# A drain of GpSimd behind every gather in a graph layer

## The chip, the cores and the metric

The kernel runs on one core of a Trainium2 chip. The metric is the device time of one execution in microseconds (us); the number that counts is the median of several executions.

## The reference

A graph of 6250 nodes with 64 features each and 206250 edges, sorted by their target node. Each node's row is normalised and clipped at zero (`h`); each edge takes its source's row of `h`, adds its own 64 attributes and clips again; the results are summed per target node, and a two-layer network with a residual closes the layer.

```python
h = jnp.maximum(_layernorm(x, axis=-1), 0.0)
# _L0_gnn_ref(h, edge_index, edge_attr, W1, b1, W2, b2):
msg = jax.nn.relu(h[src] + edge_attr)                       # 206250 x 64
agg = jax.ops.segment_sum(msg, dst, num_segments=6250)      # dst is sorted
y = jax.nn.relu((h + agg) @ W1 + b1) @ W2 + b2
out = x + y
```

## The kernel before, in words

The edges are cut into groups of 768 (128 partitions by 6 columns). Groups from the sixth on are taken in 144 **sets** of one or two groups; a set is the unit of the main loop `both_units(k)`, which lasts some 8 us. The source rows `h[src]` of a set come in two ways:

- **A little over half of the columns by matmuls.** VectorE (DVE) builds zero-one matrices (`found`, L564, and `backs`, L574), TensorE (PE) multiplies them with the table of nodes held on the chip (`across_of` L594, `turn_of` L604, `pick` L618, `decode_sum` L690), and ScalarE (ACT) copies the results out of PSUM in between (L599, L612, L683).
- **The others by gathers.** GpSimd (POOL in the profile) issues indirect DMAs from `gather` (L226): one instruction for each column, which fetches 128 rows of 64 floats out of `h_rows` in DRAM by the indices in `src_sb` and puts them into a tile `xg`. Sets of one group have no gathered column; the others have six. The first five groups are gathered whole: 18 gathers of raw rows of `x` and 12 of `h_rows`, into the tiles `xr`.

`decode(k)` adds both kinds of rows to the edges' attributes (L698 for the picked ones, L701 for the gathered ones), `messages` clips them (L708), `window_sum` (L722) sums them by target node, and `sum_into_z` (L645) adds the sums to `z`. Every so often 512 nodes go through the two-layer network (L748, L758).

The order on each engine is the order in which the code is written (a manual schedule). Two mechanisms set when a gather may start. One is written out: `fetch_next(it)` is called from inside `pick` and issues the next gather of a list `pending`, with a dependency on the matmul `it` just issued, so that the gathers are strewn among the matmuls of the main loop. The list begins nine sets ahead of the set at work (`AHEAD = 9`), and the tiles `xgs` are a ring of 11 sets. The other comes from the framework: a gather's landing is told by one of eight semaphores taken in turn, and a wait for the gather eight places earlier stands ahead of each gather as an event semaphore on POOL's sequencer.

```python
            if (u * H + t) % 2 == q // QW and q % QW == QW - 1 and (u * H + t) % (2 * H) < 2 * H - 1:
                fetch_next(it)
```

A last branch of the program (from L1114 on) handles edges that fit no window, gathers included; it is not taken with these inputs.

Of the kernel before, what the change touches and what calls it, by code (L numbers as in the profile page):

```python
# [80 lines left out]
def kernel(  # L81
# [14 lines left out]
    nc = tc.nc  # L96
# [129 lines left out]
    def gather(xg, idx, n, rows, behind=()):  # L226

        for j in range(n):
            it = nc.gpsimd.indirect_dma_start(  # L229
                out=xg[:, j, :], out_offset=None, in_=rows[:, :],  # L230
                in_offset=bass.IndirectOffsetOnAxis(ap=idx[:, j:j + 1], axis=0))
            if j >= n - len(behind):
                tc.add_manual_dep(it.ins, behind[j - n + len(behind)].ins.name, beat, reason="pace")

# [6 lines left out]
    def fetch(g, behind=()):  # L241
        lo, hi = first_col(g), pool_cols(g)
        if hi:
            gather(rows_of(g)[:, lo:], src_sb[:, g * G + lo:g * G + hi], hi - lo, x if g < RAW else h_rows, behind[lo:])
# [18 lines left out]
    def fetch_next(behind):  # L263
        if pending:
            g, j = pending.pop(0)
            gather(rows_of(g)[:, j:], src_sb[:, g * G + j:], 1, h_rows, [behind])
# [847 lines left out]
    with tc.If(any_left > 0):  # L1114
        nc.gpsimd.iota(wide, pattern=[[1, WB]], base=1, channel_multiplier=0, allow_small_or_imprecise_dtypes=True)
        with tc.For_i(0, NG, 1) as i:
            idx = work.tile([P, G], I32, name="idx")
            lf = work.tile([P, G], F32, name="lf")
            nc.vector.tensor_copy(idx, src_sb[:, ds(i * G, G)])
            nc.vector.tensor_copy(lf, left[:, ds(i * G, G)])  # L1120
            ea = eas[0][:, 0]
            nc.sync.dma_start(out=ea.rearrange("p j d -> p (j d)"),
                              in_=edge_attr[ds(i * GE, GE), :].rearrange("(p j) d -> p (j d)", j=G))
            xa = xgs[0].rearrange("p g j d -> p (g j) d")
            gather(xa, idx, G, h_rows)
            all_windows(combine(xa, ea, G), lf, G)
        ea = eas[0][:, 0]
        attr_load(ea, NG)
        xa = xgs[0].rearrange("p g j d -> p (g j) d")
        gather(xa[:, G - CT:], src_sb[:, CP - CT:], CT, h_rows)  # L1130
        all_windows(combine(xa[:, G - CT:], ea[:, G - CT:], CT), left[:, CP - CT:], CT)

        for c in range(NB + 1):
            o, xb = result(c, *hidden(c))
            base_rows(c, xb)
            store(c, o, xb)
# [39 lines left out]
```

## Time and profile before

| | |
|---|---|
| median of 3 runs | 1317.23 us (1314.55 to 1322.07) |
| the profiled execution | 1329.39 us |
| its span, first to last instruction | 1327.7 us |
| granted TensorE clock, mean | 0.918 |
| busy: PE, DVE, ACT, POOL | 1041.3, 855.2, 853.0, 764.3 us |
| gathers executed | 748 (18 + 12 into `xr`, 718 into `xg`) |

In the profile's rows a group of instructions stands as: line, engine, operation, tile written and tiles read, count; then busy time and the mean duration of one in ns; then the idle time of the engine just ahead of them and what ended it. A name with a "q" behind it (POOLq) is the engine's sequencer, which waits, branches and issues; its records are not counted as busy. A gather's record on POOL is the time in which GpSimd works on it, not the time until its rows have landed.

### The profile page before, as it was taken

To read this page: it belongs to the slowest core of one execution; us is meant where nothing else is said; L and a number is where in the kernel's file an instruction comes from. 1 tells how busy PE (TensorE), PEld (TensorE's weight loads), DVE (VectorE), ACT (ScalarE), POOL (GpSimd) and SP (SyncE) were. 2 spreads that over 40 slices of the span, in tenths; PEclk is the share of its full clock that TensorE was granted. 3 is DMA by queue.
4 is the path that set the end of the run, shared out by engine and by line. 5 is a ranking of instruction groups with operands and counts; after the bars stand their busy time and mean duration, and the time that the engine had idled before them with its cause. 6 is when DMAs were issued, how large, how long until landed. Compare 5 with 4: busy or idle time off the path is not lost. (4 is left out here: it accounts for less than half of the span.)

```text
span 1327.7 us, 39109 instructions
## 1 busy us (share of the span) xinstructions
PE 1041.3 (78%) x15593; PEld 925.0 (70%) x15593; DVE 855.2 (64%) x2167; ACT 853.0 (64%) x1849; POOL 764.3 (58%) x763
## 2 busy tenths in 40 slices
PE   0235888878887887888888888888888887888897
PEld 0224777777776777777777777777777776777796
DVE  8672766666576676576566665665666765766684
ACT  3334666666666666666666666666666666666685
POOL 7674665655565665565565565655566666566510
PEclk9767988989999999899998998989889999999898
DMA  5222444444444444444444444444444444444441
GB/s 187 81 60 93 141 134 128 144 134 122 144 138 135 146 139 134 142 119 134 130 139 140 137 138 127 138 129 139 137 139 141 139 138 141 138 139 141 127 127 55
DMA packets 92790, 173.72 MB, mean 131 GB/s; under 512 B 23673, under 2 KB 61178, under 8 KB 92602
## 3 DMA queue, kind: packets, MB, share of 16 engines
q1 hardware_dynamic: 68554, 146.58, 33.4%
q0 software_dynamic: 23936, 24.56, 9.3%
q8 instruction: 124, 2.03, 0.6%
q14 instruction: 64, 0.52, 0.2%
q10 hardware_dynamic: 112, 0.03, 0.0%
HBM read 167.22 MB, written 3.87 MB: 129 GB/s over the span
## 5 line engine op out<-in xcount | busy, mean ns | idle before, releaser
L229 POOL DMA_INDIRECT xg<-h_rows,src_sb x718 | 730.9, 1018 | 494.1 <-PE pick L618 209.3
L618 PE MATMUL pick<-picked,backs 128*128 128x128 f16 x5184 | 412.2, 230 | 35.3 <-issue 33.8
L618 PEld LDWEIGHTS <-backs 128*128 128x128 f16 x5184 | 329.8, 103 | 61.1 <-issue 50.3
L612 ACT CAST picked<-half 128x512 f16<-128x512 f32 x432 | 249.1, 577 | 177.8 <-remote 53.2
L698 DVE SCALAR_TENSOR_TENSOR ea<-pick,ea 128x192 f32<-128x192 f32 x288 | 101.7, 354 | 401.6 <-PE pick L722 108.1
L599 ACT CAST across<-half 128x512 f16<-128x512 f32 x432 | 253.7, 587 | 158.7 <-PE pick L618 57.4
L594 PE MATMUL half<-found,hp 128*128 128x128 f16 x3456 | 288.4, 229 | 22.9 <-issue 19.9
L594 PEld LDWEIGHTS <-hp 128*128 128x128 f16 x3456 | 233.8, 103 | 39.5 <-issue 31.0
L574 DVE TENSOR_SCALAR backs<-spots,ids 128x1536 f16<-128x1536 int16 x432 | 255.2, 637 | 0.0
L722 PE MATMUL pick<-oh,ea 128*64 128x32 f32 x3176 | 143.2, 226 | 82.1 <-issue 60.2
L722 PEld LDWEIGHTS pick<-oh,ea 128*64 128x64 f32 x3176 | 117.8, 138 | 118.3 <-issue 88.1
L604 PE MATMUL half<-ident_h,across 128*128 128x128 f16 x1728 | 179.4, 229 | 18.0 <-ACT across L599 13.7
L683 ACT CAST both<-pick 128x384 f16<-128x384 f32 x288 | 140.1, 486 | 62.9 <-issue 17.6
L564 DVE TENSOR_SCALAR found<-sources,nodes_of 128x1536 f16<-128x1536 int16 x288 | 170.3, 638 | 9.7 <-issue 9.7
L604 PEld LDWEIGHTS <-across 128*128 128x128 f16 x1728 | 131.0, 103 | 27.2 <-ACT across L599 14.4
L708 ACT ACTIVATE ea<-ea 128x768 f32<-128x768 f32 x144 | 114.5, 795 | 0.7 <-DVE ea L701 0.7
L684 ACT ACTIVATE minus<-both 128x192 f16<-128x192 f16 x288 | 104.5, 363 | 9.1
L655 DVE TENSOR_TENSOR oh<-slot,pick 128x384 f32<-128x384 int16 x144 | 74.0, 514 | 0.3 <-PE pick L690 0.3
L690 PE MATMUL pick<-both,weigh_high 128*128 128x192 f16 x288 | 72.6, 252 | 0.2 <-ACT both L683 0.2
L690 PE MATMUL pick<-minus,weigh_sign 128*128 128x192 f16 x288 | 72.3, 251 | 0.4 <-issue 0.3
L690 PE MATMUL pick<-both,ident_h 128*128 128x192 f16 x288 | 72.5, 252 | 0.0
L690 PE MATMUL pick<-minus,weigh_last 128*128 128x192 f16 x288 | 72.0, 250 | 0.0
(135 smaller groups left out, 809.1 us busy)
## 6 DMA issues: line engine op xcount, KB each, us to landing
sources<-source_row SPq DMA_DIRECT2D x72, 768.0 KB
ea<-in_edge_attr_dram SPq DMA_DIRECT2D x118, 384.0 KB
spots<-spot_rows SPq DMA_DIRECT2D x72, 384.0 KB
xg<-h_rows,src_sb POOLq DMA_INDIRECT x718
ea<-in_edge_attr_dram SPq DMA_DIRECT2D x32, 192.0 KB
xb<-in_x_dram SPq DMA_DIRECT2D x12, 128.0 KB
out_dram<-o SPq DMA_DIRECT2D x12, 128.0 KB
h_rows<-x SPq DMA_DIRECT2D x3, 384.0 KB
```

What stands on the lines that cost most here:

```text
L229: it = nc.gpsimd.indirect_dma_start(out=xg[:, j, :], out_offset=None, in_=rows[:, :], in_offset=bass.IndirectOffsetOnAxis(ap=idx[:, j:j + ...
L564: nc.vector.tensor_scalar(found[d][:, b * PARTS + m:b * PARTS + m + PARTS // 2].rearrange("p m u s -> p (m u s)"), sources[d][:, m * 4 * S ...
L574: nc.vector.tensor_scalar(backs[d][:, q, w].rearrange("p t s -> p (t s)"), spots[d].bitcast(I16), ids[:, w * QW + q:w * QW + q + 1], None, ...
L594: last = nc.tensor.matmul(ps[:, j * P:(j + 1) * P], hp[:, b * PARTS + m].rearrange("p t d -> p (t d)"), found[d][:, b * PARTS + m].rearran ...
L599: nc.scalar.copy(across[d, q].rearrange("p u j s -> p j u s"), ps.rearrange("p (j u s) -> p j u s", j=J, u=4))
L604: last = nc.tensor.matmul(ps[:, u * P:(u + 1) * P], ac[:, u].rearrange("p j s -> p (j s)"), ident_h, start=True, stop=True)
L612: nc.scalar.copy(picked[d][:, q].rearrange("p u d -> p (u d)"), turned.pop((d, q)))
L618: it = nc.tensor.matmul(ps[:, :, t], backs[d][:, q % QW, q // QW, u * H + t, :], picked[d][:, q, u].rearrange("p (w d) -> p w d", w=2), st ...
L683: nc.scalar.copy(both[:, i], picks_of(k, i))
L690: nc.tensor.matmul(picks_of(k, i)[:, 0], weights, rows, start=(j == 0), stop=(j == len(terms) - 1))
L708: nc.scalar.activation(msg, msg, AF.Relu)
L722: last = nc.tensor.matmul(pa[i * D:(i + 1) * D], msg[:, j, :], oh[:, j, :], start=(j < lo + 2), stop=(j >= G - 2))
```

## The change

Behind every indirect DMA that `gather` issues, a drain is put into GpSimd's instructions: a step of its sequencer that is meant to wait until the engine has finished the instructions before it. All calls of `gather` are affected: the 748 that run and the ten in the branch that is not taken. The semaphores, the waits, the dependencies of the pace and the order of all other instructions on all engines stay as they were; the drains themselves wait for no semaphore and set none.

```diff
@@ def gather(xg, idx, n, rows, behind=()):
             it = nc.gpsimd.indirect_dma_start(
                 out=xg[:, j, :], out_offset=None, in_=rows[:, :],
                 in_offset=bass.IndirectOffsetOnAxis(ap=idx[:, j:j + 1], axis=0))
+            nc.gpsimd.drain()
             if j >= n - len(behind):
                 tc.add_manual_dep(it.ins, behind[j - n + len(behind)].ins.name, beat, reason="pace")
```

## The prediction

> **What bounds the kernel now.** I read the page first, for shares and for the chain that ended last.
>
> ```profile
> span 1327.7 us, 39109 instructions
> PE 1041.3 (78%) x15593; PEld 925.0 (70%) x15593; DVE 855.2 (64%) x2167; ACT 853.0 (64%) x1849; POOL 764.3 (58%) x763
> PE 39%; issue 7%; ACT 2%; DVE 1%; DMA 0%; DVEq 0%; POOL 0%; ACTq 0%
> ```
>
> The third row is the chain by engine. It was followed back over only half of the span (its shares sum to 49%), but in that half PE holds 39 of 49 and POOL nothing. PE is the bound, with the engines that feed it out of PSUM; POOL, which the change touches, is busy for 58% and off the path. So the question is how far POOL can be slowed before somebody waits for its gathers. Next I read POOL's one large group in the main loop alone (121 to 1268.5 us), and the page of the gather's line, in which the last two rows are those who waited for it.
>
> ```profile
> L229 POOL DMA_INDIRECT xg<-h_rows,src_sb x676 | 686.2, 1015 | 471.8 <-PE pick L618 209.3 <-issue 77.6 <-PE half L604 68.4
> L229 POOL DMA_INDIRECT xg<-h_rows,src_sb x718: 938/944/1732, 43.6 to 1267.4; - x180
> L229 POOLq EVENT_SEMAPHORE  x699: 17/17/3868, 27.0 to 1265.6; - x175
> ...
>   ACT raw_sq L630: 5.9, 1
>   POOL xr L229: 0.6, 2
> ```
>
> 676 gathers of 1015 ns make 686.2 us of work in that stretch, and POOL idles 471.8 us ahead of them, mostly because the pace (the pick at L618 and its neighbours) has not let the next one go. Nobody in the main loop is shown waiting for a gather; the two rows of waiters lie in the first 60 us. How early the gathers are is read from their reader, the addition at L701:
>
> ```profile
> L701 DVE SCALAR_TENSOR_TENSOR ea<-xg,ea x120: 544/559/568, 133.8 to 1316.3; 128x384 f32<-128x384 f32 x120
> ...
>   issue: 0.6, 2
> ```
>
> Idle time of DVE ahead of 120 of these is 0.6 us in all. Now the ends of the loop on POOL's timeline (start, duration, what, idle time ahead of it), and a step of the chain that shows a gather's landing:
>
> ```profile
> 51.64 0.94 POOL L229 DMA_INDIRECT xg<-h_rows,src_sb  x1 [1.62 <-DVE raw_v L633]
> ...
> 109.34 0.94 POOL L229 DMA_INDIRECT xg<-h_rows,src_sb  x1 [0.30 <-issue]
> 121.07 1.54 POOL L229 DMA_INDIRECT xg<-h_rows,src_sb  x1 [10.79 <-PE pick L618]
> ...
> 1151.08 0.95 POOL L229 DMA_INDIRECT xg<-h_rows,src_sb  x1 [0.30 <-issue]
> 1152.33 0.94 POOL L229 DMA_INDIRECT xg<-h_rows,src_sb  x1 [0.31 <-issue]
> ...
> 1267.40 0.94 POOL L229 DMA_INDIRECT xg<-h_rows,src_sb  x1 [0.45 <-PE pick L690]
> ```
>
> ```profile
> 1151.08 3.33 DMA xg<-h_rows,src_sb
> ```
>
> The gather at 51.64 is the sixth into `xg`, the last one that the first L701 (133.8) needs: it ended 81 us early. The last one ends at 1268.34 and the last L701 starts at 1316.3: 48 us early. A gather lands some 3.33 us after its start, 2.4 after its end, so the cushion is 79 us at first and 45.6 at the end. And two gathers that wait for nothing stand 0.30 us apart: already now they don't overlap.
>
> **The change, part by part.** It adds 748 drains to POOL's sequencer and touches nothing else. Behind a drain are queued the next event semaphore (the 17 ns row) and the next gather; who waits for those is L701 alone, with the cushion above.
>
> *The price of one drain.* No drain behind a gather is in the trace; these are the drains there are, with the last of four MEMSETs that the first of them stands behind:
>
> ```profile
> L1162 POOLq DRAIN  x1: 188/188/188, 0.4 to 0.4; - x1
> ...
> 0.41 0.12 POOL L1162 MEMSET const-uint8-127<- 128x1 uint8 x1
> ...
> L1171 POOLq DRAIN  x3: 40/107/9212, 1301.0 to 1327.4; - x3
> L1171 SPq DRAIN  x3: 7/7/13, 1326.8 to 1327.1; - x3
> ...
> L1114 POOLq INC_SWDGE_SEM  x1: 2426/2426/2426, 1298.6 to 1298.6; - x1
> ```
>
> POOL's drain at 0.4 ran 188 ns, to about 0.59, and the MEMSET ended at 0.53: it lets go within 0.1 us of the engine's end. The two cheap ones at the program's end cost 40 and 107 ns with POOL idle. The long one (9212 ns, at 1301.0) follows a step on DMA semaphores that itself took 2426 ns and stands behind no gather; I read it as the wait for that step. So a drain adds at most 0.107 us of its own beyond the gather's end in the ordinary rows.
>
> Then the restart: with a drain the sequencer can no longer hand over the next gather while the present one runs. What an instruction costs that starts behind an engine that has just come to rest:
>
> ```profile
> 0.82 0.20 POOL masks.py:197 MEMSET ident<- 128x128 f32 x1 [0.29 <-POOLq L1162]
> 1.10 0.29 POOL masks.py:199 TENSOR_SCALAR_AFFINE_SELECT ident<-ident 128x128 f32<-128x128 f32 x1
> ...
> 3.50 0.14 POOL L186 IOTA nodes_of<- 128x3 f32 x1
> 3.82 1.10 POOL L229 DMA_INDIRECT xr<-in_x_dram,src_sb  x1 [0.19 <-issue]
> ```
>
> The select at 1.10 starts 0.08 us behind the end (1.02) of the MEMSET whose result it needs; the first gather starts 0.19 us behind an IOTA. Both are less than the 0.30 us that lie between gathers anyway. I add X to that gap. Lower bound: 0, if drain and restart fit inside the 0.30 us. Upper bound: 0.107 (drain) + 0.017 (event semaphore) + a whole further 0.305 us gap = 0.43 us, if nothing of today's gap overlaps with them. I take 0.107 + 0.017 + 0.08 = 0.20 us, since the select behind the MEMSET is the nearest row of a restart that had to wait for the engine's own end. Below nothing the price cannot go: today's gap is the same for gathers that were let go long before.
>
> The Trainium skill has the rule for this on its page "PSUM — Partial Sum Buffer", section "Engine vs sequencer instructions": a drain waits until its engine is fully idle. The page "VectorE: DVE Perf Modes", section "The DRAIN you can't avoid", gives the boilerplate drains as a constant 12 ns or so on all five engines. By that figure the drains would cost POOL 748 x 12 ns, an estimate of 9 us in all; SP's 7 to 13 ns agree with it, while POOL's 40, 107 and 188 ns do not, and the measured ones decide.
>
> *Does POOL have room?* In the main loop the idle time beyond the fixed gaps is 471.8 - 676 x 0.305 = 266 us, or 0.39 us a gather. With X = 0.20 the drains take 135 us of it. Idle time is uneven, so I also replayed POOL's 748 gathers one by one, each starting at its old start or at the end of the one before plus 0.305 + X, whichever is later: with 0.20 no gather is later than 6.8 us, and the last one ends 0.1 us later than now. Against a cushion of 45.6 us or more that is nothing. The point from which someone waits: from 121.07 to the last L701 less the landing (1313.9) there are 1192.8 us for 676 gathers; the replay has the first of them 11 us late at such an X; (1192.8 - 11) / 676 = 1.75 us each, less 1.015 and 0.305, leaves X = 0.43 us. That is the upper bound of the price, so the whole range of X is hidden. The cover is PE's pace; without it every gather would cost 0.20 us, 150 us in all.
>
> *The start*, where there is less cushion. The raw gathers feed the first messages; the tightest are the second group and the fifth (the last gather of each, then DVE's first reading of it):
>
> ```profile
> 18.04 1.50 POOL L229 DMA_INDIRECT xr<-in_x_dram,src_sb  x1 [0.30 <-issue]
> 40.63 0.54 DVE L625 TENSOR_REDUCE raw_s<-xr 128x6 f32<-128x384 f32 x1
> ...
> 42.33 0.94 POOL L229 DMA_INDIRECT xr<-h_rows,src_sb  x1 [0.30 <-issue]
> 67.37 0.54 DVE L491 SCALAR_TENSOR_TENSOR ea<-xr,ea 128x384 f32<-128x384 f32 x1
> ```
>
> The first lands at about 19.5 + 2.4 = 21.9 and is read at 40.63: 18.7 us early, and 11 drains ahead of it make it 2.2 us later (4.7 at 0.43). The other lands at 45.7, is read at 67.37, and is 5.8 us later (12.5 at 0.43). Hidden too; the ACT wait of 5.9 us that the page puts down to a gather reads `xr` behind DVE's subtraction, and the gathers into `xr` are over at 43.3.
>
> *The sum* is 0 on the profiled execution's 1327.7 us span (1329.39 us in all). The profiled execution is 12.2 us above the median of the runs, so the forecast stands on the median: **1317 us**. The extra instructions to be fetched (748 beside some 7900 that are not PE's) ride on a DMA queue with 0.2% of the engines' time, and cost nothing.
>
> **The rivals.**
>
> *POOL becomes the bound by the drain's own price.* If drain and restart cost more than 0.43 us together (GpSimd may do work behind the gather's recorded end that a drain has to wait out), the lag grows set by set, uses up the cushion near the end, and each further 0.01 us costs 6.8 to 7.5 us. At X = 0.50 the replay has the last gather 51.1 us too late for its L701, plus 2.4 for the landing: 1317 + 54 = 1371 us; at 0.60 it is 1445. For it: the unexplained 9212 ns. Against it: the next gather starts 0.305 us behind the recorded end today, so hidden work cannot be longer than that, and with it the price just reaches the point. Chance 0.12.
>
> *The drain waits until the rows have landed.* Then a gather follows the one before by 3.33 + 0.31 = 3.64 us; 748 of them make 2723 us, with 3.8 ahead and 11.4 from the last L701 to the end 2738, some 2726 on the median's scale. It decides from the first set on, as a period of 3.64 us needs more than twice POOL's room of 1.75. For it: "fully idle" may include the transfers. The page "Perfetto Trace Analysis" of the Trainium skill, section "DMA Instruction — SWDGE (GPSIMD)", ends a gather's work on GpSimd with the last descriptor written and has the data move later, which speaks against it; no run here shows which of the two a drain sees. Against it in the trace: the eight landing semaphores are watched by event semaphores, not by the engine. Chance 0.09. A drain that behaves like the 9212 ns row behind every gather would give 748 x 10.5 = 7900 us; I give that 0.02.
>
> *The drain does nothing on GpSimd's gathers* and goes by in about 10 ns as on SP. Then the time is the same, 1317 us; I count 0.10 for it, inside the forecast.
>
> *Faster.* The mean gather takes 1015 ns, the least 938: 77 ns x 748 = 58 us in which gathers are held up by something beside them. If that something were held up as well and the drains moved the gathers off it, an engine would gain; but DVE, the likeliest, holds 1 of 49 parts of the chain, about 1 us of the 58. Chance of over 0.5%: 0.05.
>
> **How the numbers follow.** About 0.5% (6.6 us) is what a measurement of this kernel can tell from no change; its three runs spread over 0.57%. Forecast hidden, X from 0 to 0.43, with the drain that does nothing: 0.68, as "same". Faster 0.05. Slower: 0.12 + 0.09 + 0.02, and 0.04 for a small loss that I cannot name: 0.27. The forecast's own range is 1310 to 1324. For 8 in 10 the range takes in part of the first rival, up to X = 0.50, and leaves out the landing and the worst: 1309 to 1372.
>
> **What would show it right or wrong.** Right: rows of POOLq DRAIN x748 at L229; the smallest gap between gathers grows from 0.30 to about 0.50 us; POOL's busy time stays near 764 us; its waits on PE at L618 shrink; the last gather still ends near 1268; L701 still waits for nothing. Wrong: a gap of 0.75 us or more, POOL without waits for PE, L701 or DVE waiting for a gather's landing, the span following POOL's period times 748.

## The result, and the profile after

The changed kernel takes 2774.8 us (median of 4 runs, 2763.2 to 2786.6) against 1319.65 us before (4 runs): 2.10 times as long, with a 95% interval of 2.09 to 2.11. The experiments below ran on four chips; on three of them the kernel before takes 1006 us and not 1320, so each is compared with the kernel before on its own chip.

First the page of the changed kernel (line numbers are one higher from the drain on): span, busy shares, the chain by engine, POOL's group of gathers and DVE's addition that reads them.

```profile
span 2761.4 us, 39857 instructions
PE 1166.7 (42%) x15593; PEld 1070.1 (39%) x15593; DVE 850.5 (31%) x2167; ACT 869.2 (31%) x1849; POOL 745.2 (27%) x763
...
issue 65%; POOLq 33%; PE 1%; DMA 0%; POOL 0%; DVE 0%; ACT 0%; DVEq 0%
...
L229 POOL DMA_INDIRECT xg<-h_rows,src_sb x718 | 713.1, 993 | 1923.2 <-issue 966.1
...
L702 DVE SCALAR_TENSOR_TENSOR ea<-xg,ea 128x384 f32<-128x384 f32 x120 | 67.0, 558 | 1664.8 <-DMA xg<-h_rows,src_sb 1664.8
```

The chain has left PE and lies on POOL's sequencer, yet POOL is busy for no more time than before (745 against 764 us). What has grown is the idle time ahead of its gathers. The same row on the page of the kernel before:

```profile
L229 POOL DMA_INDIRECT xg<-h_rows,src_sb x718 | 730.9, 1018 | 494.1 <-PE pick L618 209.3
```

(713.1 + 1923.2) / 718 = 3.67 us from one gather to the next; before it was (730.9 + 494.1) / 718 = 1.71. And the reader that waited for nothing now waits for a gather's landing before nearly every set: 1664.8 us. The drains' row, the landing of the gathers, and three periods of POOL's timeline with the same stretch of the chain:

```profile
L232 POOLq DRAIN  x748: 2352/2763/11783, 3.5 to 2746.4; - x187
```

```profile
DMA to landing us min/median/max: 2.3/2.5/11.5
```

```profile
1500.64 0.95 POOL L229 DMA_INDIRECT xg<-h_rows,src_sb  x1 [2.32 <-issue]
1503.97 0.95 POOL L229 DMA_INDIRECT xg<-h_rows,src_sb  x1 [2.38 <-issue]
1507.17 0.95 POOL L229 DMA_INDIRECT xg<-h_rows,src_sb  x1 [2.26 <-issue]
```

```profile
1500.43 1.16 POOLq L232
1501.59 1.67 issue
1503.26 0.02 POOLq L229
1503.27 0.48 issue
1503.75 1.16 POOLq L232
```

The sequencer takes up the drain at 1500.43, just ahead of the gather's recorded start at 1500.64. The gather's work on GpSimd is over at 1501.59; the drain is not. Its record runs 2.786 us, to 1503.21. The last of the 16 updates of that gather's landing semaphore came at 1503.14. I took this difference for all 748 pairs of records: the drain ends 0.072 us behind the landing, always between 0.072 and 0.081, whether the landing took 2.3 us or 11.5. Then come the event semaphore (1503.26), half a microsecond in which the sequencer takes up the next gather, and the gather at 1503.97, 0.76 us behind the drain's end.

That is the whole time. On the mean over the 748 a gather lands 2.84 us after its start; 2.84 + 0.07 + 0.76 = 3.67 us. 747 such periods are 2743 us, from the first gather at 3.83 to the last at 2746.66, and 14.8 us follow to the end of the span. PE's granted clock is lower too (0.703 on the mean instead of 0.918, and 257 ns for a pick's matmul instead of 230), but PE has 58% of the span free and holds 1% of the chain, so this does not set the time.

### The profile page after: what moved, and what is told of

Read it like the earlier page. It is cut to its first block, busy times and chain, and to the rows that moved or that the text cites. A ratio compares the mean times of both kernels' runs of the same rounds, so it can differ in the third digit from the quotient of the medians.

```text
span 2761.4 us, 39857 instructions
## 1 busy us (share of the span) xinstructions
PE 1166.7 (42%) x15593; PEld 1070.1 (39%) x15593; DVE 850.5 (31%) x2167; ACT 869.2 (31%) x1849; POOL 745.2 (27%) x763
## 4 chain that ended last, share of the span: by engine, by line
issue 65%; POOLq 33%; PE 1%; DMA 0%; POOL 0%; DVE 0%; ACT 0%; DVEq 0%
POOLq L232 33%; POOLq L229 1%; DMA xg<-h_rows,src_sb 0%; PE pick L619 0%; POOL xg L229 0%; PE half L595 0%; PE pick L723 0%; PE half L759 0%; POOL xr L229 0%; PE pick L691 0%; PE half L605 0%; PE rows L749 0%; DVE ea L702 0%; ACT ea L709 0%; DVE oh L656 0%
## 5 line engine op out<-in xcount | busy, mean ns | idle before, releaser
L229 POOL DMA_INDIRECT xg<-h_rows,src_sb x718 | 713.1, 993 | 1923.2 <-issue 966.1
L619 PE MATMUL pick<-picked,backs 128*128 128x128 f16 x5184 | 473.0, 257 | 1428.8 <-DVE z L646 1428.8
L619 PEld LDWEIGHTS <-backs 128*128 128x128 f16 x5184 | 406.5, 118 | 1455.3 <-issue 1446.3
L702 DVE SCALAR_TENSOR_TENSOR ea<-xg,ea 128x384 f32<-128x384 f32 x120 | 67.0, 558 | 1664.8 <-DMA xg<-h_rows,src_sb 1664.8
L595 PE MATMUL half<-found,hp 128*128 128x128 f16 x3456 | 310.7, 242 | 0.9 <-DVE found L565 0.8
L595 PEld LDWEIGHTS <-hp 128*128 128x128 f16 x3456 | 259.5, 111 | 19.1 <-issue 16.1
L605 PE MATMUL half<-ident_h,across 128*128 128x128 f16 x1728 | 198.8, 247 | 0.9 <-ACT picked L613 0.6
L605 PEld LDWEIGHTS <-across 128*128 128x128 f16 x1728 | 151.2, 114 | 4.5 <-ACT picked L613 0.8
L723 PE MATMUL pick<-oh,ea 128*64 128x32 f32 x3176 | 122.4, 226 | 25.9 <-ACT ea L709 25.7
L691 PE MATMUL pick<-both,weigh_high 128*128 128x192 f16 x288 | 89.1, 309 | 0.2 <-ACT both L684 0.2
```

The lines of the kernel that those rows point to most:

```text
L229: it = nc.gpsimd.indirect_dma_start(out=xg[:, j, :], out_offset=None, in_=rows[:, :], in_offset=bass.IndirectOffsetOnAxis(ap=idx[:, j:j + ...
L595: last = nc.tensor.matmul(ps[:, j * P:(j + 1) * P], hp[:, b * PARTS + m].rearrange("p t d -> p (t d)"), found[d][:, b * PARTS + m].rearran ...
L605: last = nc.tensor.matmul(ps[:, u * P:(u + 1) * P], ac[:, u].rearrange("p j s -> p (j s)"), ident_h, start=True, stop=True)
L619: it = nc.tensor.matmul(ps[:, :, t], backs[d][:, q % QW, q // QW, u * H + t, :], picked[d][:, q, u].rearrange("p (w d) -> p w d", w=2), st ...
L691: nc.tensor.matmul(picks_of(k, i)[:, 0], weights, rows, start=(j == 0), stop=(j == len(terms) - 1))
L723: last = nc.tensor.matmul(pa[i * D:(i + 1) * D], msg[:, j, :], oh[:, j, :], start=(j < lo + 2), stop=(j >= G - 2))
```

## The experiments

The numbers behind an experiment's name are its runs and the time of the kernel before on its chip. Of each edit only the lines inside `gather` are shown; the names that they use (`issued`, `after`, `mark`, `data`) are set up just above it. Where such lines are added the gather stands on L231 or L232.

**Two drains behind every gather** (one run; 1006.0 us before).

```diff
+            nc.gpsimd.drain()
             nc.gpsimd.drain()
```

> Two drains behind every gather instead of one. Theory 1, a drain waits until the rows of the gathers before it have landed: the second drain finds them landed and costs its idle price, 40 to 107 ns by the drains at the program's ends, with some 50 ns around it, so the period of the gathers goes from 3.67 to 3.75-3.85 us and the time to 2820-2900 us. Theory 2, a drain is a fixed piece of GpSimd's own work of some 2.8 us: the period goes to 6.4 us and the time to about 4830 us.

2841.4 us. The first and the second drain in the profile of that kernel:

```profile
L232 POOLq DRAIN  x748: 2372/2772/11384, 3.5 to 2824.7; - x187
```

```profile
L233 POOLq DRAIN  x748: 41/41/41, 11.9 to 2827.4; - x187
```

All 748 second drains cost 41 ns. A drain of GpSimd that finds nothing under way costs next to nothing; theory 2 is out. The changed kernel itself, run on another chip of that kind, took 2790.6 us with 1005.9 us before:

> The changed kernel on the same chip as the experiments. Theory 1: it is bound by 748 gathers in a row, landing 2.84 us + 0.07 us to the drain's end + 0.76 us to the next start = 3.67 us each, whatever PE's speed: 2740-2790 us, as on the first chip, although the kernel before differs by 31% between the two.

That is 0.6 us above the range: a gather lands 2.88 us after its start here, and the period is 3.71 us. So the time is that of the gathers in a row, hardly moved by a chip on which the kernel before takes 24% less time.

**A wait for the landing, without a drain** (one run; 1006.0 us before).

```diff
+            if issued:
+                tc.add_manual_dep(it.ins, issued[-1].ins.name, data, reason="landing")
+            issued.append(it)
```

> No drain; each gather waits for the landing semaphore of the gather just before it instead of the eighth before it. Theory 1: the same limit without any drain, a landing of 2.84 us from the start (mean with drains) and a restart of at most 0.76 us, 3.4-3.65 us a gather, 2560-2750 us. Theory 2: without the drain's own work only the landing and today's gap of 0.31 us remain, 3.15 us a gather or less, 2370 us or less.

2697.4 us, near the upper end of theory 1's range, with no drain in the kernel. From its page and from the list of those who waited for the gathers:

```profile
L232 POOL DMA_INDIRECT xg<-h_rows,src_sb x718 | 714.8, 996 | 1867.6 <-DMA xg<-h_rows,src_sb 975.2
...
  DVE ea L707: 1608.1, 119
```

(714.8 + 1867.6) / 718 = 3.60 us a gather, and DVE waits for landings almost as long as with drains. Here the wait is mostly an event semaphore on the sequencer, and the next gather starts 0.71 us behind it (704.281 to 704.995 in one place), 0.74 us behind the landing in 689 of the 747 periods. In 50 others the gather itself holds the wait, and it starts 0.26 us behind the landing. (In the kernel before, too, 43 gathers hold their wait for the gather eight places earlier themselves.) The drain is thus worth a full wait for the landing, and 0.10 us more: 0.83 us from the landing to the next start on the mean, against 0.73 here.

**A wait for the engine, but not for the landing**, and its control without the wait (one run each; 1006.0 us before; the first again in two runs).

```diff
+            if after:
+                tc.add_manual_dep(it.ins, after[-1].ins.name, data, reason="restart")
+            after.append(nc.gpsimd.memset(mark, 0.0))
```

> No drain; behind each gather stands a MEMSET of one column on GpSimd, and the next gather waits for that MEMSET's semaphore. So the sequencer may not hand over a gather before the one ahead is done on the engine, but nobody waits for a landing. The prediction's price for this (at most 0.43 us on top of today's gap): hidden, 1310-1325 us. Theory 3, the restart of a gather costs the 0.76 us that the trace with drains shows between a drain's end and the next gather's start: 0.99 + 0.1 + 0.76 = 1.85 us a gather or somewhat more, above the 1.75 us for which there is room, so POOL bounds the loop and the time is 1400-1500 us.

> The control for the one before: the same MEMSET behind each gather, but the next gather does not wait for it. All theories: the gathers are handed over ahead as before, the MEMSET adds 0.1-0.3 us to a period of 1.3 us, below the room of 1.75 us, and the time stays at 1310-1325 us.

1158.9 us with the wait and 1012.0 without it, 1006.0 before. The rows of both on their pages (with the wait, then the control):

```profile
L232 POOL DMA_INDIRECT xg<-h_rows,src_sb x718 | 746.9, 1040 | 204.4 <-POOL mark L237 95.3
...
L237 POOL MEMSET mark<- 128x1 f32 x748 | 147.6, 197 | 0.8
```

```profile
L232 POOL DMA_INDIRECT xg<-h_rows,src_sb x718 | 721.0, 1004 | 82.9 <-issue 31.4
...
L235 POOL MEMSET mark<- 128x1 f32 x748 | 191.2, 256 | 0.3
```

From start to start over all gathers the period is 1.525 us with the wait and 1.326 without: the wait costs 0.20 us. The gather starts 0.27 us behind the MEMSET's end in 741 of 747 places. In 558 of the 747 the MEMSET takes 0.11 us, and the gap between two gathers is 0.385 us, 0.08 more than without the wait; in the other 189 it takes 0.41 us, and the gap is 0.68. The gathers are 0.04 us longer as well. So the restart behind the engine's own end would fit inside the 0.305 us that lie between gathers anyway; what is paid is the MEMSET's own time and the longer gathers. The prediction's X of 0.20 us was thus not too low for a wait of this kind. That the mean comes to the same 0.20 is luck: there is no drain here, and the terms are others. Theory 3's 1.85 us is out for this form of wait: the gather itself holds it, as in the 50 places of the kernel with the wait for the landing, and the half microsecond in which the sequencer takes up a gather is saved. (The expectation's times were written for a chip with 1317 us; the periods decide.) It is not hidden here, because on this chip POOL has no room. The kernel before, profiled on such a chip:

> The kernel before, profiled again, since on the chip of the experiments it took 1006 us against 1317 us where the change was measured. Expected if that chip simply leaves PE fewer stops: gathers unchanged in length (0.94 us at least, 0.30 us apart), but a set is shorter, so that POOL's idle time beyond the fixed gaps falls from 266 us to near nothing, and the granted clock is near 0.98 instead of 0.918. Time 1000-1010 us on that chip, 1310-1330 us on a chip like the first.

```profile
span 1004.4 us, 39109 instructions
PE 918.9 (91%) x15593; PEld 848.7 (84%) x15593; DVE 874.7 (87%) x2167; ACT 849.2 (85%) x1849; POOL 754.4 (75%) x763
...
L229 POOL DMA_INDIRECT xg<-h_rows,src_sb x718 | 720.8, 1004 | 219.0 <-PE pick L618 49.4
```

1006.1 us. The idle time of 219.0 us is 718 fixed gaps of 0.305 us and nothing more (none of them is longer than 0.317, so the PE that the row names held no gather up): gathers run back to back at 1.31 us, with PE at 91%. In two more runs, with an expectation for both kinds of chip, the kernel with the wait came out at 1161.4 us, 1.153 times before (1.150 to 1.156; 1007.4 us before).

> The MEMSET and the wait for it once more, to see it on another chip. The wait costs a gather 0.2 us (period 1.525 us against 1.326 with the MEMSET alone). Where the kernel before takes about 1320 us, a gather has 1.75 us of room and the wait is hidden: within 1% of before, as the prediction worked it out for a drain that lets go at the engine's end. Where the kernel before takes about 1006 us there is no room: 1150-1165 us as before.

It met no chip of the first kind again, so that 0.20 us a gather would be hidden where 1.75 us are to be had is argued, not shown.

**A drain behind every second gather** (one run; 1005.9 us before).

```diff
+            issued.append(it)
+            if len(issued) % 2 == 0:
+                nc.gpsimd.drain()
```

> A drain behind each second gather only. Theory 1: a pair takes 1.25-1.3 us for the gather that is not drained and 3.67 us for the drained one, 4.95 us; 374 pairs make 1850 us, with 3.8 us ahead and 11-14 behind 1860-1880 us. If the loss did not come from the gathers in a row on POOL but from a few places in the loop, the time would not follow the number of drains.

1963.8 us, 4.5% above the upper end of theory 1's range. From its page:

```profile
L231 POOL DMA_INDIRECT xg<-h_rows,src_sb x718 | 710.0, 989 | 1153.6 <-issue 410.9
```

A gather takes 2.60 us, a pair 5.2 instead of the expected 4.95. The term that was off most is the landing: the second gather of a pair lands 3.02 us after its start on the mean, not 2.84, and the drain ends 0.11 us behind that, not 0.07; with the next start 0.77 us later 1.30 + 3.02 + 0.11 + 0.77 = 5.20. Half of the drains cost 958 us where all of them cost 1785 on the same chip, so the loss is spread over them and does not come from a few places.

**Drains behind the first 30 gathers only** (one run, then two more; 1005.9 and 1007.4 us before).

```diff
+            issued.append(it)
+            if len(issued) <= 30:
+                nc.gpsimd.drain()
```

> Drains behind the first 30 gathers only, those that fetch whole groups at the program's start. Theory 1: they end some 70 us later (113.5 us with drains, 43.3 without); their readers have about 22 us of cushion, so that the main loop starts 40-60 us later, and the time is 1006 + 40 to 60 us, 1045-1070 us on the chip where the kernel before takes 1006 us. The prediction's reading (the start is hidden): no loss.

> Drains behind the first 30 gathers once more. They end 70 us later; where the kernel before takes about 1320 us, the loop has room to catch up but its start is later: 1320 + 40 to 60 us; where it takes about 1006 us, 1065-1070 us as before.

1067.9 us, then 1070.9 (1.063 times before, 1.060 to 1.066), the second 0.9 us above its range. On POOL's timeline of the first run, the end of the drained stretch:

```profile
110.58 0.94 POOL L231 DMA_INDIRECT xr<-h_rows,src_sb  x1 [2.34 <-issue]
113.80 1.04 POOL L231 DMA_INDIRECT xg<-h_rows,src_sb  x1 [2.28 <-DVE ea L496]
115.14 1.31 POOL L231 DMA_INDIRECT xg<-h_rows,src_sb  x1 [0.30 <-issue]
```

The first gather into `xg` starts at 113.80 instead of 43.8, and behind the last drain the gap is 0.30 us again. Of the 70 us that POOL is late 62 come out at the end: 30 of the 748 drains cost 62 us here.

**Two and three gathers under way** (one run each; 1322.7 us before), as the wait for the landing, with `issued[-2]` and `issued[-3]`.

> No drain; each gather waits for the landing of the gather two before it, so that two may be under way at once. Theory 1 (what the drain costs is that only one gather is under way): a landing of 2.85 us and a restart of 0.73 us are shared by two gathers, 1.8 us each, 748 of them 1340 us, with what lies ahead and behind 1350-1400 us. If a wait on a gather's landing cost a fixed amount for each gather, it would stay near the 2697 us of the kernel with one under way.

> No drain; each gather waits for the landing of the gather three before it. Theory 1: 3.58 / 3 = 1.19 us a gather, less than the 1.31 us at which GpSimd makes them anyway, so that the wait is hidden for all but the late landings: 1006-1060 us where the kernel before takes 1006 us.

1583.2 and 1374.7 us. The gathers' rows of the two pages:

```profile
L232 POOL DMA_INDIRECT xg<-h_rows,src_sb x718 | 731.0, 1018 | 775.6 <-DMA xg<-h_rows,src_sb 282.1
```

```profile
L232 POOL DMA_INDIRECT xg<-h_rows,src_sb x718 | 725.7, 1011 | 530.7 <-PE pick L624 166.9
```

With two under way a gather takes 2.10 us, not 1.8, and the time is 13% above the range. By the records of the DMA packets a gather's last packet ends 2.80 us after its start on the mean, against 2.49 with one under way (on a chip of the other kind). If the landing is longer by the same 0.31 us, that makes (2.85 + 0.31 + 0.73) / 2 = 1.95 us, an estimate; the rest is not explained. With three POOL is back at waiting for PE, 1.75 us a gather against 1.71 in the kernel before, and DVE's waits for gathers, 1608 us with one under way and 527 with two, are down to 0.6 us. From one to two to three under way the period falls from 3.60 to 2.10 to 1.75 us, so it is the number of gathers under way that the drain takes away. The last one is 52 us (4%) slower than its kernel before. That is within the 0 to 54 us expected, on the other kind of chip, for late landings; but as DVE does not wait for gathers here, the cause stays open.

## Why the prediction was wrong

It forecast 1317 us with a range of 1309 to 1372 and a chance of 0.68 for no change; 2774.8 us is far outside.

**The step that failed is the price of one drain.** The prediction bounded it by 0.43 us from a drain behind a MEMSET (188 ns, gone 0.05 us behind the MEMSET's end) and from two on an idle engine. All three stand behind instructions that end on the engine. A gather's record ends on the engine as well, but its rows are still under way, and the drain waits for those. The measured X is 3.67 - 1.31 = 2.36 us, more than five times the upper bound. The argument that hidden work cannot be longer than the 0.305 us to the next gather failed with it: gathers that are not drained follow each other at 1.31 us while a landing takes 2.84, so the rows of one are under way while the next is at work.

**The row that was put aside.** The drain of 9212 ns was read as the wait for the step on the DMA semaphores ahead of it. The rows of the same two instructions at the end of the changed kernel:

```profile
L1115 POOLq INC_SWDGE_SEM  x1: 185/185/185, 2750.6 to 2750.6; - x1
```

```profile
L1172 POOLq DRAIN  x3: 40/53/107, 2750.9 to 2761.1; - x3
```

With 748 drains behind the gathers, the one at the end costs 53 ns and the step ahead of it 185. With drains behind the first 30 only they are 6746 and 1815 ns; without drains 9212 and 2426 in all eight runs. So both have to do with gathers that had not been drained, but not with their landing: they are as long in the kernel that waits for every landing, and in the kernel before the row begins 32.7 us after the last gather's work has ended. What they do, and whether the drain only waits for the step ahead of it, stays open. The row could not have told the price that was missed.

**The rival that came true** is the landing, with a chance of 0.09 and a time of 2726 us, 2% under the result. Its period of 3.64 us had a landing of 3.33 us, read from one step of the chain, and the gap of 0.31 of the kernel before; the parts are 2.84, 0.07 and 0.76 us. The errors cancelled. The two arguments against it did not hold: that event semaphores watch the landing semaphores says nothing of what a drain watches, and a gather's record ending with the engine's work is not where a drain ends. The page "Perfetto Trace Analysis" of the Trainium skill (section "DMA Instruction — SWDGE (GPSIMD)") ends such a record with the last descriptor and not with the data; the trace agrees, as records of 0.95 us end 1.5 us ahead of the median landing. The rule of the Trainium skill's page "PSUM — Partial Sum Buffer" (section "Engine vs sequencer instructions"), that a drain waits for a fully idle engine, must on GpSimd be read with the transfers that the engine has issued; the 0.072 us show it.

**What held.** The room (1.75 us a gather on that chip, and the cushion) decides as worked out: a period of 3.67 us is beyond it, and DVE's L702 became the waiter. A wait for the engine's own end is cheap: 0.27 us behind the MEMSET, inside the gap that is there anyway. That it came to 0.20 us a gather in all, the prediction's X, is luck. That the start is hidden fell with the price: 2.3 us a drain instead of 0.20 make the raw gathers 70 us late, against some 20 us of cushion.

## What to carry to other kernels

A wait costs what it waits for, not what its own record takes on an idle engine: before pricing a drain, ask what its engine still has under way, transfers included, and where no row shows it with something under way, treat its price as open. Transfers as short as these need several under way (one at a time cost 3.60 us a gather, three 1.75); a step that allows only one turns the landing into the period. And where an engine is the pace of the loop, even 0.2 us an instruction is paid in full.

## What the runs showed of the hardware

- A drain of GpSimd behind an indirect DMA ends 0.072 us after the rows have landed (748 of 748 within 0.01 us); behind the second of two, 0.11 us after (374 of 374). A drain right behind the first takes 41 ns.
- If the sequencer itself was held (by a drain, or by an event semaphore ahead of the gather), the next gather starts 0.71 to 0.76 us later; if the gather held the wait, it started 0.26 us behind a landing (50 places) and 0.27 us behind a MEMSET's end (741 places).
- A gather alone landed 2.84 us after its start on the mean (median 2.5), but 3.02 us as the second of two.
- The same kernel before takes 1317 to 1323 us in two of the sets of runs and 1006 to 1007 in three others, at granted clocks of 0.92 to 0.93 and of 0.98. What sets the difference is open.
